# A modulated four-layer residual convolution: a block sum moved from GpSimd to VectorE, a scaled identity moved from VectorE to ScalarE

## The chip, the cores and the metric

The kernel runs on one core of one Trainium2 chip. The metric is device time in microseconds, the median of several executions. All work is in 32-bit floats.

## What is computed

The reference passes a batch of 128 samples (64 channels, 1024 columns) through four modulated convolutions and adds the input. Cut to what matters:

```
for i, typ in enumerate(('same', 'upsample', 'same', 'downsample')):
    s = style @ mw.T + mb
    weight = SCALE * w * s[:, None, :, None]
    demod = rsqrt(sum(weight * weight, axis=(2, 3)) + EPS)
    weight = weight * demod[:, :, None, None]      # one weight per sample
    out = conv(x, weight) + b                      # 3 taps; up and down with a blur
...
return x + out
```

## The kernel before

**One combined convolution per sample.** All four layers are linear, so the kernel multiplies the layers' weights of each sample into one chain on TensorE, and then applies one short convolution to the input; the ends of the rows are done apart. Samples go in quartets, 32 of them (q = 0 to 31). Four samples share a tile: two halves of the partitions times two positions in the free dimension. [...]

**The chain of a quartet.** `scale3` makes tile wd (third layer's weights, scaled). `stage1` multiplies it with the second-layer weights into PSUM tile psS, and ScalarE copies that, scaled by table tB, into tile S, which holds eight blocks (slots) of 64 columns. Quartets 0, 1, 2 and 6 use the plain `stage1`. The other 28 use `stage1_a` and `stage1_b`: five products by way of sums of neighbouring taps; ScalarE writes four slots, VectorE (L442) two more from PSUM, and GpSimd (L445) adds slot 0 to slot 2. `share_sums` (L462) adds slots pairwise. `stage2` multiplies S with the blurred first layer E into psR, in turns that share through `share`, `share_copy` and `stage2_rest`, with differences of E's taps in Ed; ScalarE copies the result as tile R (scaled by tC). `stage3` multiplies R with the zeroth layer into the tile W, called Wf in the profile, scaled by table t0. From quartet 6 it is split in `stage3_b` and `stage3_a`: after stage3_b ScalarE copies two blocks from psA to psW in four operations, then five blocks to Wf in two; stage3_a adds to psW, and ScalarE copies four blocks more.

**From the weights to the output.** `combine_a` and `combine_b` make on VectorE (all at L662, the helper `sum_of`) the three sums h1, h2, h3 of the weights, tile H in the profile. Between h1 and h3 `residual` (L659) adds to one tap, for each half r, the identity matrix divided by three, idn3, times the sample's entry of table t3: this is the `x +` of the reference. `combine_a` makes h1, the residual, and h3; `combine_b` h2, h1, and h2 again. `product` (L753) does the convolutions: conv3 needs only h3, conv1 and conv2 need h1 and h2, conv4 and conv0 need W itself. Input sums T and G come from VectorE and GpSimd. ScalarE copies conv3's result (m3), VectorE makes y1 (`sum1`) and the third outputs Y (`sum2`: first Y = 3 m3 + psA, in one operation for each of two PSUM banks, then y1 less psA). conv4 then adds to Y. `output` scales on ScalarE, SyncE's queue stores.

**The order of the work** is written out by hand and kept: each engine executes its instructions in the order of the program. `early_turn` serves q = 0 to 3, `turn_of` q = 4 to 28, and the last three quartets stand at the end. Turn q finishes quartet q, makes the combined weights of n = q + 1 and the chain of c = q + 2. In `turn_of` the order is stage2(c), conv2(q), sum2(q), stage3_b(c), combine_a(n), conv4(q), stage3_a(c), combine_b(n), conv3(n), outputs, copies, conv0(q), conv1(n). In the first of these turns (q = 4, entry) sum2, conv4 and combine_a(n) stand ahead of stage3_b, and r_sums(c) (L588) on VectorE behind combine_a. In the turn at q = 29 it is stage2, conv2, stage3 part 0, sum2's first step, combine_a(n), conv4, conv3. In an early turn it is stage2(c), sum2(q), combine_a(n), conv4(q), stage3(c, 0), conv3(n).

Of the kernel before, what the change touches and what calls it, by code (L numbers as in the profile page):

```python
# [63 lines left out]
def kernel(  # L64
# [199 lines left out]
    def var_newton(bs, ls=slice(0, NL)):  # L264
# [4 lines left out]
    ALT, ODD, DOWN = slice(0, 4, 2), slice(1, 4, 2), (slice(3, 4), slice(1, 2))  # L269
    tA, tB, tBn, tC, t0, t3, td, tb = (  # L270
        const.tile([P, NQ, 2], F32, name=n) for n in ("tA", "tB", "tBn", "tC", "t0", "t3", "td", "tb")
    )
# [20 lines left out]
    def table_B(bs):  # L293
        table(nc_g, tB, bs, ALT, DOWN, sc[:, 2, bs], sc[:, 1, bs])

    def table_Bn(bs):
        qs = slice(bs.start // 4, bs.stop // 4)
        nc_g.tensor_scalar_mul(tBn[:, qs], tB[:, qs], -1.0)

# [65 lines left out]
    w3x = const.tile([P, 5, C], F32, name="w3x")  # L365
    w2n = const.tile([P, 5, C], F32, name="w2n")

    def split_weights():
        nc_g.tensor_copy(w3x[:, :K], w3)
        nc_g.tensor_scalar_mul(w2n[:, :K], woi[2], -1.0)  # L370
        for t, src in ((w3x, w3), (w2n, woi[2])):
            nc_g.tensor_add(t[:, K:], src[:, : K - 1], src[:, 1:])

# [30 lines left out]

    EVEN = slice(0, K, 2)

    def stage1(q, pool=None, engs=(nc_a, nc_a), between=None):

        wd = chain[q]
        ps = unit(pool or ps_w, f"psS{q}")  # L410
        for k, (at, at1) in enumerate(((0, 3), (3, 1), (1, 4))):
            tap_matmul(ps, wd, at, 2, woi[2][:, k, :], EVEN, first=k == 0)
            tap_matmul(ps, wd, at1, 1, woi[2][:, k, :], slice(1, 2), last=k == K - 1)
        if between:
            between()
        st, _ = s_tiles(q)
        for r in range(2):
            scaled_copy(engs[r], flat(st[r][:, 1:6]), ps[r][:, : 5 * C], tB[:, q, r : r + 1])
        chain[q] = st
        return ps  # L420

    def stage1_a(q, ps=None):

        ps = ps or unit(ps_w, f"psS{q}")
        wd = chain[q]
        tap_matmul(ps, wd, 2, 2, w2n[:, 0, :], EVEN, first=True)
        tap_matmul(ps, wd, 3, 2, w2n[:, 2, :], EVEN)
        tap_matmul(ps, wd, 1, 1, w2n[:, 1, :], slice(1, 2))
        st, t = s_tiles(q)
        for r in range(2):  # L430
            scaled_copy(nc_a, flat(st[r][:, :4]), ps[r][:, C : 5 * C], tBn[:, q, r : r + 1])
        chain[q] = wd, ps, st, t

    def stage1_b(q):

        wd, ps, st, t = chain[q]
        tap_matmul(ps, wd, 2, 1, w2n[:, 3, :], slice(3, 4))
        tap_matmul(ps, wd, 4, 1, w2n[:, 4, :], slice(4, 5), last=True)
        for r in range(2):
            p1 = st[r][:, 0:1, :].to_broadcast([P, 2, C])  # L440
            sums = ps[r][:, 2 * C : 6 * C].rearrange("c (a b o) -> c a b o", a=2, b=2)[:, :, 0]
            nc_v.scalar_tensor_tensor(  # L442
                st[r][:, 4:6, :], sums, tB[:, q, r : r + 1], p1, op0=ALU.mult, op1=ALU.subtract
            )
        nc_g.tensor_add(t[:, :, 2], t[:, :, 2], t[:, :, 0])  # L445
        chain[q] = st
        whole[q] = t
# [5 lines left out]
    def tap_differences():  # L453

        d = Ed[:, :4].rearrange("c (a b) o -> c a b o", a=2)
        for b in range(2):
            nc_g.tensor_sub(d[:, :, b], E[:, 4 * b : 4 * b + 5 : 4], E[:, 2:7:4])
        nc_g.tensor_sub(Ed[:, 4:], E[:, 3:8:4], E[:, 5:6].to_broadcast([P, 2, C]))

    def share_sums(q):  # L460
        t = whole[q]
        nc_v.tensor_add(t[:, :, 6:8], t[:, :, 1:5:3], t[:, :, 2:6:3])  # L462

# [12 lines left out]
    def share(q, ps):  # L476

        at = [NB + 4 + i * C for i in range(3)]
        p12, p34 = ([b[:, i:j] for b in ps] for i, j in zip(at, at[1:]))
        chain_matmul(p12, E[:, 2], chain[q], slice(6, 7))  # L480
        chain_matmul(p34, E[:, 6], chain[q], slice(6, 7))
        chain_matmul(p34, E[:, 5], chain[q], slice(7, 8), True)
        shared_ps[q] = [b[:, at[0] : at[2]] for b in ps]
# [12 lines left out]
    def stage2_rest(q):  # L496
# [4 lines left out]
        plan = (  # L501
            (apart, E[:, 0], slice(1, 4, 2)),
            (block(1), Ed[:, 0], slice(2, 3)),
            (block(2), Ed[:, 1], slice(1, 2)),
            (block(3), E[:, 2], slice(3, 4)),
            (block(3), Ed[:, 2], slice(2, 3)),
            (block(4), Ed[:, 3], slice(1, 2)),
            (block(4), E[:, 4], slice(3, 4)),
            (block(5, 2), E[:, 8], slice(2, 4)),
            (block(5), E[:, 6], slice(3, 4)),  # L510
            (block(1, 2), E[:, 1], slice(4, 6)),
            (block(2), E[:, 3], slice(4, 5)),
            (block(3), Ed[:, 4], slice(5, 6)),
            (block(4), Ed[:, 5], slice(4, 5)),
            (block(5), E[:, 7], slice(5, 6)),
        )
# [4 lines left out]
    def stage2(q, pool=None, engs=(nc_a, nc_a), between=None):  # L521
# [3 lines left out]
        for n, e in enumerate(() if shared else (-2, -1, 0, 1, 2, 3, 4, 5, 6)):  # L525
            if e % 2 == 0:
                a, lo, m = slice(1, 4), e // 2 + 1, 3
            else:
                a, lo, m = slice(4, 6), (e + 3) // 2, 2
            for r, rows in enumerate(HALF):  # L530
                for c, cols in enumerate(HALF):
                    src = st[c if r == 0 else 1 - c]
                    nc.tensor.matmul(  # L533
                        ps[r][cols, lo * C : (lo + m) * C],
                        E[rows, e + 2, :],
                        src[rows, a, :],
# [90 lines left out]
    def stage3(q, part, pool=None, engs=(nc_a, nc_a)):  # L627
# [24 lines left out]
        return ps  # L652

    def residual(q):

        W = Wq[q][0]
        for r in range(2):
            v = W[:, tap(1, 1), r, :]
            nc_v.scalar_tensor_tensor(v, idn3, t3[:, q, r : r + 1], v, op0=ALU.mult, op1=ALU.add)  # L659

# [207 lines left out]
    w0s = [woi[0]] + [const.tile([P, K, C], F32, name=f"w0s{i}") for i in range(2)]  # L868
    idn3 = const.tile([P, C], F32, name="idn3")

    def scaled_weights():
# [308 lines left out]
    stage3(0, 1, ps_conv, BOTH)  # L1180
    const_first(0, first)
    stage1(2)
    combine_a(0)
# [21 lines left out]
    for of in (table_B, vector_a1, table_0, vector_b1, vector_c2):  # L1205
        of(PART[1])
    table_Bn(slice(0, PART[1].stop))
    stage3(1, 1)
# [38 lines left out]
    def layers(i, j):  # L1247
# [5 lines left out]
        (2, 1): lambda: (small_rest(2), var_root(REST, Y[:, 0])),  # L1253
        (2, 2): lambda: (table_B(REST), table_Bn(REST), vector_a1(REST)),
        (3, 0): lambda: (var_newton(*layers(2, 3)), var_newton(*layers(0, 2))),
# [381 lines left out]
```

## Time and profile before

| what | value |
|---|---|
| median of 3 runs | 479.15 us (478.75 to 479.64) |
| profiled execution, its own time from first to last instruction | span 478.0 us |
| the median less that span | 1.15 us |
| share of the span: TensorE, VectorE, ScalarE, GpSimd | 98%, 87%, 65%, 34% |
| TensorE, convolutions psA from T and H (L753) | 2304 passes, 187.3 us |
| VectorE, residual (L659) | 64 operations, 16.9 us, 304 ns each |
| GpSimd, sum in S (L445) | 28 operations, 22.1 us, 790 ns each |
| VectorE, sums from PSUM into S (L442) | 56 operations, 16.8 us, 341 ns each |

PE in the profile is TensorE's matrix work, PEld its loading of weights, DVE VectorE, ACT ScalarE and POOL GpSimd. A row of the timeline has the start, the length, the engine, the line, the operation with what it writes and reads, and the count of merged rows; in brackets stands how long the engine had been idle and who released it. A row of the groups has the total busy time, the mean of one in ns, and then the idle time before. Neighbouring operations of one engine overlap a little, so two of 0.31 us can start 0.21 apart.

### The profile page before, as it was taken

How to read it: one execution, taken by the hardware profiler on the slowest of the kernel's cores; microseconds unless marked ns; L12 is line 12 of the kernel's file. 1: busy time of each engine (PE TensorE's matmuls, PEld its weight loads, DVE VectorE, ACT ScalarE, POOL GpSimd, SP SyncE). 2: the span in 40 equal slices, each digit the busy share in tenths (PEclk: the TensorE clock that was granted, in tenths of full speed). 3: DMA queues.
4: the chain of work that ended last, by engine and by line, in shares of the span. 5: the costliest groups of instructions: out<-in, count | busy, mean ns of one | idle time of the engine just before them, and what ended most of it. 6: DMA issues, size and time to landing. Idle time of an engine off the chain costs nothing.

```text
span 478.0 us, 26721 instructions
## 1 busy us (share of the span) xinstructions
PE 469.6 (98%) x11928; PEld 346.4 (72%) x11928; DVE 417.5 (87%) x690; ACT 310.1 (65%) x708; POOL 163.5 (34%) x197
## 2 busy tenths in 40 slices
PE   8999999999999999999999999999999999999995
PEld 7877788777878876677776677766887777766652
DVE  5889998879889998899979899979989999999895
ACT  5565666667666676666667666667666768766352
POOL 3434032663335342243432233422434432333200
PEclk9999999999999999999999999999999999999998
DMA  5406365544445554345543455533455554445125
GB/s 175 158 28 200 114 195 192 150 139 144 139 150 157 173 173 127 122 151 160 171 149 120 131 170 152 173 127 126 145 169 162 162 154 146 152 146 170 61 91 191
DMA packets 50514, 70.70 MB, mean 148 GB/s; under 512 B 5664, under 2 KB 47328, under 8 KB 50400
## 3 DMA queue, kind: packets, MB, share of 16 engines
q1 hardware_dynamic: 49808, 68.32, 45.8%
q8 instruction: 93, 1.52, 1.5%
q10 hardware_dynamic: 592, 0.69, 0.5%
q14 instruction: 21, 0.17, 0.1%
HBM read 35.36 MB, written 33.62 MB: 144 GB/s over the span
## 4 chain that ended last, share of the span: by engine, by line
PE 95%; DVE 4%; issue 0%; ACT 0%; ACTq 0%; DVEq 0%
PE psA L753 45%; PE Y L753 11%; PE psR L467 9%; PE psA L571 7%; PE psW L571 7%; PE psS L389 6%; PE psR L533 4%; PE psA L467 2%; PE Y L994 2%; DVE H L662 1%; PE Y L180 1%; PE Y L336 1%; DVE G L662 0%; PE psM L204 0%; DVE o L832 0%
## 5 line engine op out<-in xcount | busy, mean ns | idle before, releaser
L753 PE MATMUL psA<-T,H 64*64 64x340 f32 x2304 | 187.3, 447 | 0.8 <-DVE y L662 0.7
L753 PEld LDWEIGHTS psA<-T,H 64*64 64x64 f32 x2304 | 89.9, 133 | 50.0 <-issue 3.1
L662 DVE SCALAR_TENSOR_TENSOR G<-X 128x1376 f32<-128x1376 f32 (+2 forms) x65 | 78.1, 1207 | 1.1 <-DMA X<-in_x 0.9
L726 POOL TENSOR_TENSOR T<-G 128x684 f32<-128x684 f32 x28 | 46.5, 1659 | 73.1 <-DVE G L662 73.1
L445 POOL TENSOR_TENSOR S<-S 128x128 f32<-128x128 f32 x28 | 22.1, 790 | 144.1 <-ACT S L360 136.8
L360 ACT ACTIVATE R<-psR,tC 128x448 f32<-128x448 f32 x63 | 36.5, 630 | 46.3 <-PE psR L467 26.7
L753 PE MATMUL psA<-T,Wf 64*64 64x340 f32 x768 | 63.9, 446 | 0.0
L753 PE MATMUL Y<-T,Wf 64*64 64x340 f32 x768 | 62.8, 451 | 0.1
L662 DVE SCALAR_TENSOR_TENSOR Y<-m,psA 128x340 f32<-128x340 f32 x64 | 33.1, 517 | 28.0 <-PE psA L753 26.6
L360 ACT ACTIVATE psW<-psA 128x128 f32<-128x128 f32 x100 | 19.3, 269 | 50.3 <-PE psA L571 46.2
L740 DVE TENSOR_TENSOR T<-G 128x1368 f32<-128x1368 f32 (+1 forms) x33 | 50.7, 1540 | 0.0
L360 ACT ACTIVATE Wf<-psW,t 128x256 f32<-128x256 f32 (+2 forms) x76 | 32.7, 479 | 26.5 <-PE psW L571 26.2
L711 DVE TENSOR_TENSOR T<-X 128x684 f32<-128x684 f32 x32 | 47.9, 1496 | 0.0
L467 PE MATMUL psR<-S,E 64*64 64x64 f32 (+1 forms) x1472 | 46.5, 238 | 0.0
L731 POOL TENSOR_TENSOR T<-G 128x684 f32<-128x684 f32 x28 | 46.5, 1660 | 0.0
L389 PEld LDWEIGHTS psS<-wd,w2n 64*64 64x64 f32 x1120 | 35.0, 133 | 13.3 <-ACT S L360 0.8
L467 PEld LDWEIGHTS psR<-S,E 64*64 64x64 f32 x1472 | 39.6, 134 | 5.2 <-ACT psR L490 0.2
L753 PEld LDWEIGHTS Y<-T,Wf 64*64 64x64 f32 x768 | 29.6, 132 | 18.0 <-DVE Y L662 0.7
L830 ACT ACTIVATE o<-psA,tb,td 128x340 f32<-128x340 f32 x63 | 37.0, 647 | 6.3 <-PE psA L753 6.3
L753 PEld LDWEIGHTS psA<-T,Wf 64*64 64x64 f32 x768 | 29.1, 133 | 15.1
L830 ACT ACTIVATE o<-Y,tb,td 128x340 f32<-128x340 f32 x63 | 36.6, 637 | 4.5 <-PE Y L753 2.7
L830 ACT ACTIVATE o<-y,tb,td 128x340 f32<-128x340 f32 x62 | 38.5, 679 | 0.6 <-DVE y L812 0.6
(165 smaller groups left out, 832.4 us busy)
## 6 DMA issues: line engine op xcount, KB each, us to landing
out<-o SPq DMA_DIRECT2D x167, 170.0 KB, 2.6
X<-in_x SPq DMA_DIRECT2D x150, 172.0 KB, 3.6
X<-in_x SPq DMA_DIRECT2D x14, 516.0 KB, 5.3
out<-o SPq DMA_DIRECT2D x6, 510.0 KB, 5.4
out<-o SPq DMA_DIRECT2D x2, 340.0 KB, 3.0
Xe<-in_x_ends SPq DMA_DIRECT2D x1, 512.0 KB, 6.7
out<-o ACTq DMA_DIRECT2D x3, 170.0 KB, 2.3
par<-in_params SPq DMA_DIRECT2D x2, 192.0 KB, 3.4
```

Source lines behind the costliest of these rows:

```text
L360: nc_a.activation(dst, src, AF.Copy, scale=f)
L389: nc.tensor.matmul(ps[r][cols, at * C : (at + n) * C], weight[rows], wd[c if r == 0 else 1 - c][rows, taps], start=first, stop=last, skip_ ...
L445: nc_g.tensor_add(t[:, :, 2], t[:, :, 2], t[:, :, 0])
L467: nc.tensor.matmul(dst[r][cols], weight[rows], st[c if r == 0 else 1 - c][rows, slots, :], start=False, stop=last, skip_group_check=True,)
L571: nc.tensor.matmul(dst[r][cols], weight[rows], t[rows, c, slots, :], start=first, stop=last, skip_group_check=True,)
L662: nc_v.scalar_tensor_tensor(out, x, f, y, op0=ALU.mult, op1=op)
L711: nc_v.tensor_sub(t[:, pairs, 0, :NJ], plane(X, 3, pairs), plane(X, 1, pairs))
L726: eng.tensor_add(t[:, :, 0, :NJ], plane(g, 2), plane(g, 1))
L731: eng.tensor_sub(t[:, :, 1, :NJ], plane(g, 2), plane(g, 1))
L740: nc_v.tensor_sub(t[:, pairs, :, :NJ], both(a, PL), both(b, 1))
L753: nc.tensor.matmul(ps[s][cols, :NB], w, Ts[q, tag][rows, c, i, g : g + NB], start=(g == 0 and m == 3), stop=(g == K - 1), skip_group_check ...
L830: nc_a.activation(dst, src, AF.Identity, bias=add, scale=d3)
```

## The change

Four things are edited.

1. **S's middle block.** `stage1_a` no longer uses negated weights and the negated table tBn; it writes the slots 0, 2, 4, 6 with tB. `stage1_b` uses negated sums w2n (now two blocks), and its VectorE operation makes three slots, 3 to 5, of 192 columns, in place of two. GpSimd's addition is gone. The odd slots stay negated, and the products of stage2 that read them use negated odd taps En; all slot numbers change, the number and sizes of the products do not.
2. **The plain stage1** multiplies all three taps of wd in one go (192 columns) instead of two and one. Its odd slots are not negated, so stage2 uses E for those quartets.
3. **The residual.** A new function `identity` makes x3, 128 columns, on ScalarE in two operations of 64, from idn3 and t3. It is called at the head of `combine_a` (for q = 0 a little earlier). `residual` is one addition of 128 columns on VectorE. x3 is one tile for all quartets.
4. **sum2's first step** is one operation over both banks where the two lie in one tile.

```
+    w2n = const.tile([P, 2, C], F32, name="w2n")
+    En = const.tile([P, 4, C], F32, name="En")
...
+        nc_g.tensor_add(w2n, woi[2][:, : K - 1], woi[2][:, 1:])
+        nc_g.tensor_scalar_mul(w2n, w2n, -1.0)
+
+    def negated_taps():
+        nc_g.tensor_scalar_mul(En, E[:, 1:8:2], -1.0)
...
-        for k, (at, at1) in enumerate(((0, 3), (3, 1), (1, 4))):
-            tap_matmul(ps, wd, at, 2, woi[2][:, k, :], EVEN, first=k == 0)
-            tap_matmul(ps, wd, at1, 1, woi[2][:, k, :], slice(1, 2), last=k == K - 1)
+        plain.add(q)
+        for k in range(K):
+            tap_matmul(ps, wd, k, K, woi[2][:, k, :], slice(0, K), first=k == 0, last=k == K - 1)
...
-            p1 = st[r][:, 0:1, :].to_broadcast([P, 2, C])
-            sums = ps[r][:, 2 * C : 6 * C].rearrange("c (a b o) -> c a b o", a=2, b=2)[:, :, 0]
+            p1 = st[r][:, 0:1, :].to_broadcast([P, K, C])
+            sums = ps[r][:, 2 * C : 5 * C].rearrange("c (a o) -> c a o", o=C)
             nc_v.scalar_tensor_tensor(
-                st[r][:, 4:6, :], sums, tB[:, q, r : r + 1], p1, op0=ALU.mult, op1=ALU.subtract
+                st[r][:, 3:6, :], sums, tB[:, q, r : r + 1], p1, op0=ALU.mult, op1=ALU.add
             )
-        nc_g.tensor_add(t[:, :, 2], t[:, :, 2], t[:, :, 0])
...
-        nc_v.tensor_add(t[:, :, 6:8], t[:, :, 1:5:3], t[:, :, 2:6:3])
+        nc_v.tensor_add(t[:, :, 1:8:6], t[:, :, 2:4], t[:, :, 4:6])
...
-            (block(1, 2), E[:, 1], slice(4, 6)),
-            (block(2), E[:, 3], slice(4, 5)),
+            (block(1, 2), En[:, 0], slice(3, 6, 2)),
+            (block(2), En[:, 1], slice(3, 4)),
...
+    def identity(q):
+        for r in range(2):
+            nc_a.activation(x3[:, r], idn3, AF.Copy, scale=t3[:, q, r : r + 1])
+
     def residual(q):
-        W = Wq[q][0]
-        for r in range(2):
-            v = W[:, tap(1, 1), r, :]
-            nc_v.scalar_tensor_tensor(v, idn3, t3[:, q, r : r + 1], v, op0=ALU.mult, op1=ALU.add)
+        v = Wq[q][0][:, tap(1, 1)]
+        nc_v.tensor_add(v, v, x3)
...
     def combine_a(q):
         chain.pop(q)
+        if q:
+            identity(q)
         a, b, c, h1, h2, h3 = taps(q)
         sum_of(h1, c, -2.0, a)
         residual(q)
...
-            for s, a in enumerate(banks(q)):
-                sum_of(Y[:, s, :NB], m3[:, s], 3.0, a[:, :NB])
+            for s, a in parts(q):
+                sum_of(Y[:, s, :NB], m3[:, s], 3.0, a)
```

More of the change, by code (lines that the diff above doesn't have):

```diff
@@ L405 @@
     EVEN = slice(0, K, 2)
+    plain = set()
     def stage1(q, pool=None, engs=(nc_a, nc_a), between=None):
@@ L501, in stage2_rest @@
         plan = (
[L502 to L510, printed above, removed]
-            (block(1, 2), E[:, 1], slice(4, 6)),
-            (block(2), E[:, 3], slice(4, 5)),
+            (apart, E[:, 0], slice(2, 7, 4)),
+            (block(1), Ed[:, 0], slice(4, 5)),
+            (block(2), Ed[:, 1], slice(2, 3)),
+            (block(3), E[:, 2], slice(6, 7)),
+            (block(3), Ed[:, 2], slice(4, 5)),
+            (block(4), Ed[:, 3], slice(2, 3)),
+            (block(4), E[:, 4], slice(6, 7)),
+            (block(5, 2), E[:, 8], slice(4, 7, 2)),
+            (block(5), E[:, 6], slice(6, 7)),
+            (block(1, 2), En[:, 0], slice(3, 6, 2)),
+            (block(2), En[:, 1], slice(3, 4)),
             (block(3), Ed[:, 4], slice(5, 6)),
-            (block(4), Ed[:, 5], slice(4, 5)),
-            (block(5), E[:, 7], slice(5, 6)),
+            (block(4), Ed[:, 5], slice(3, 4)),
+            (block(5), En[:, 3], slice(5, 6)),
         )
@@ L526, in stage2 @@
             if e % 2 == 0:
-                a, lo, m = slice(1, 4), e // 2 + 1, 3
+                a, lo, m, w = slice(2, 7, 2), e // 2 + 1, 3, E[:, e + 2]
             else:
-                a, lo, m = slice(4, 6), (e + 3) // 2, 2
+                a, lo, m = slice(3, 6, 2), (e + 3) // 2, 2
+                w = E[:, e + 2] if q in plain else En[:, (e + 1) // 2]
             for r, rows in enumerate(HALF):
@@ L1181 @@
     const_first(0, first)
+    identity(0)
     stage1(2)
@@ L1206 @@
         of(PART[1])
-    table_Bn(slice(0, PART[1].stop))
+    negated_taps()
     stage3(1, 1)
```

40 lines of the change are left out of this document (18 added, 22 removed).

## The prediction

> **What bounds the kernel now.** I read the page first, its shares, its clock row and its chain of waits:
>
> ```profile
> PE 469.6 (98%) x11928; PEld 346.4 (72%) x11928; DVE 417.5 (87%) x690; ACT 310.1 (65%) x708; POOL 163.5 (34%) x197
> PEclk9999999999999999999999999999999999999998
> PE 95%; DVE 4%; issue 0%; ACT 0%; ACTq 0%; DVEq 0%
> ```
>
> TensorE is busy for 98% of the span, at a clock that is full in all but the last slice, and 95% of the chain lies on it. So an edit pays only where it takes work from TensorE or a wait in front of it, and it costs wherever it puts a wait in front of it. Time won on VectorE, ScalarE or GpSimd is worth nothing by itself. Next I looked, in the timeline, at the part of one ordinary turn in which the changed operations stand (columns: start, length, engine, line, operation, count, and the idle time before it):
>
> ```profile
> 279.34 1.07 DVE L662 SCALAR_TENSOR_TENSOR Y<-m,psA 128x340 f32<-128x340 f32 x2 [0.76 <-PE psA L753]
> ...
> 280.15 0.21 PEld L571 LDWEIGHTS psA<-R,par 64*64 64x64 f32 x8
> ...
> 280.46 1.35 PEld L753 LDWEIGHTS Y<-T,Wf 64*64 64x64 f32 x24
> ...
> 280.73 0.77 ACT L360 ACTIVATE psW<-psA 128x128 f32<-128x128 f32 x4 [1.90 <-PE psA L571]
> 281.09 0.57 DVE L662 SCALAR_TENSOR_TENSOR H<-Wf 128x384 f32<-128x384 f32 x1
> 281.37 0.97 ACT L360 ACTIVATE Wf<-psA,t 128x320 f32<-128x320 f32 x2
> 281.59 0.47 DVE L659 SCALAR_TENSOR_TENSOR Wf<-idn,t,Wf 128x64 f32<-128x64 f32 x2
> ...
> 282.09 0.56 DVE L662 SCALAR_TENSOR_TENSOR H<-H,Wf 128x384 f32<-128x384 f32 x1
> ...
> 282.77 0.26 PEld L571 LDWEIGHTS psW<-R,w0s 64*64 64x64 f32 x8
> ...
> 282.94 1.36 PEld L753 LDWEIGHTS psA<-T,H 64*64 64x64 f32 x24
> ...
> 283.27 0.84 ACT L360 ACTIVATE Wf<-psW,t 128x256 f32<-128x256 f32 x2 [0.93 <-PE psW L571]
> ```
>
> In this stretch TensorE runs stage3_b of quartet c (until about 280.4), conv4 (weights from 280.46), stage3_a (its last weights at 282.77) and conv3 of quartet n (weights from 282.94), one straight after the other. Beside it VectorE makes the weights of conv3 in three operations: h1 at 281.09, the residual pair at 281.59 (L659), h3 at 282.09, which ends at 282.65. conv3 starts 0.29 us later, so its weights are in time, but only just. ScalarE, at the same moment, is at work for the *other* quartet c: four copies at 280.73, then two scaled ones that end at 281.37 + 0.97 = 282.34. It cannot start them earlier, since it waited 1.90 us for stage3_b of TensorE.
>
> **The change, part by part.** *The residual.* Before, L659 reads a table and needs nothing fresh from ScalarE. Now it adds x3, and ScalarE writes x3 in the same turn. The kernel's order decides how late. On ScalarE, in an ordinary turn, stood (psA, psW and Wf of quartet c):
>
> ```order
> L360 ACTIVATE psW_0_4723<-psA_4692 128x2x64
> L360 ACTIVATE psW_1_4724<-psA_4692 128x2x64
> L360 ACTIVATE Wf_4693<-psA_4692,t_137 128x5x64 x2
> L360 ACTIVATE Wf_4693<-psW_0_4723,t_137 128x4x64
> L360 ACTIVATE Wf_4693<-psW_1_4724,t_137 128x4x64
> ```
>
> and now (x_156 is x3, idn_155 the scaled identity):
>
> ```order
> L356 ACTIVATE psW_0_4660<-psA_4629 128x2x64
> L356 ACTIVATE psW_1_4661<-psA_4629 128x2x64
> L356 ACTIVATE Wf_4630<-psA_4629,t_136 128x5x64 x2
> L658 ACTIVATE x_156<-idn_155,t_137 128x64 x2
> L356 ACTIVATE Wf_4630<-psW_0_4660,t_136 128x4x64
> L356 ACTIVATE Wf_4630<-psW_1_4661,t_136 128x4x64
> ```
>
> The two identities of quartet n stand behind all copies of stage3_b of quartet c. On VectorE the residual keeps its place between h1 and h3; before:
>
> ```order
> L662 SCALAR_TENSOR_TENSOR Y<-m_16_4802,psA_4692 128x340 x2
> L812 TENSOR_TENSOR y_16_4887<-y_16_4887,psA_4692 128x680
> L662 SCALAR_TENSOR_TENSOR H_4694<-Wf_4693 128x384
> L659 SCALAR_TENSOR_TENSOR Wf_4693<-idn_155,t_138,Wf_4693 128x64 x2
> L662 SCALAR_TENSOR_TENSOR H_4694<-H_4694,Wf_4693 128x384
> ```
>
> and now:
>
> ```order
> L666 SCALAR_TENSOR_TENSOR Y<-m_16_4740,psA_4629 128x2x340
> L818 TENSOR_TENSOR y_16_4824<-y_16_4824,psA_4629 128x680
> L666 SCALAR_TENSOR_TENSOR H_4631<-Wf_4630 128x384
> L663 TENSOR_TENSOR Wf_4630<-Wf_4630,x_156 128x128
> L666 SCALAR_TENSOR_TENSOR H_4631<-H_4631,Wf_4630 128x384
> ```
>
> So a new chain leads to conv3: stage3_b on TensorE, six copies on ScalarE, two identities, the addition, h3, conv3. Queued behind the waiting addition are h3, the rest of combine_b and the turn's input sums; conv3 waits for h3, and everything that TensorE still has to do waits for conv3. The prices come from these rows:
>
> ```profile
> L462 DVE TENSOR_TENSOR S<-S 128x256 f32<-128x256 f32 x23 | 9.6, 418 | 0.0
> L255 DVE TENSOR_TENSOR nw<-dm,var 128x64 f32<-128x64 f32 x2 | 0.4, 222 | 0.0
> L442 DVE SCALAR_TENSOR_TENSOR S<-psS,tB,S 128x128 f32<-128x128 f32 x56 | 16.8, 341 | 5.4 <-ACT o L830 2.8 <-PE psS L389 2.3
> L360 ACT ACTIVATE psW<-psA 128x128 f32<-128x128 f32 x100 | 19.3, 269 | 50.3 <-PE psA L571 46.2 <-issue 4.1
> L662 DVE SCALAR_TENSOR_TENSOR Y<-m,psA 128x340 f32<-128x340 f32 x64 | 33.1, 517 | 28.0 <-PE psA L753 26.6
> L662 DVE SCALAR_TENSOR_TENSOR y<-psA,m 128x680 f32<-128x680 f32 x32 | 27.6, 862 | 7.4 <-PE psA L753 5.9 <-PE psW L571 1.3
> ```
>
> and from the timeline near the start of the kernel:
>
> ```profile
> 16.24 0.42 ACT L360 ACTIVATE Wf<-psW,t 128x192 f32<-128x192 f32 x1 [0.15 <-PE Y L914]
> 16.70 0.42 DVE L362 TENSOR_SCALAR Wf<-psW,t 128x192 f32<-128x192 f32 x1 [0.50 <-ACT Wf L360]
> ...
> 33.64 0.31 ACT L245 ACTIVATE dm<-Y,eps 128x64 f32<-128x64 f32 x1 [0.98 <-PE Y L232]
> 33.85 0.31 ACT L247 ACTIVATE var<-Y,eps 128x64 f32<-128x64 f32 x1
> ```
>
> Two 128x64 activations with a pointer operand start 0.21 us apart, so each identity moves the end on ScalarE by 0.21: the pair ends at 282.34 + 0.42 = 282.76. VectorE starts 0.04 after ScalarE's end (16.66 to 16.70). The addition of 128x128 lies between the 222 ns of 128x64 and the 418 ns of 128x256, on the line 0.29. h3 follows 0.03 later (282.06 to 282.09) and takes 0.56; weights are loaded 0.05 after VectorE's end (279.34 + 1.07 = 280.41 to 280.46). Sum: 282.34 + 0.42 + 0.04 + 0.29 + 0.03 + 0.56 + 0.05 = 283.73, against 282.94 now: **0.79 us of waiting in a turn**. Nothing hides it: all of TensorE's later work stands behind conv3, and the next turn's copies again start only when TensorE has done stage3_b, so no lead is carried over. The bounds: two identities at the 0.17 spacing of the four copies at 280.73 ((0.77 - 0.27) / 3), or a little under, 0.30, with an addition of 0.22, give 0.60; two without overlap, 0.62, and an addition of 0.34 (L442) give 1.04.
>
> The Trainium skill (ScalarE: Activation LUTs, section "What ACT_TABLE_LOAD costs") gives an ACTIVATE 186 ns + 0.833 ns an element, 93 ns more for a pointer operand, and 93 ns of overlap between neighbours. By that an identity is about 332 ns and a pair moves the end by 0.48 in place of 0.42, an estimate that would make the sum below 1.4 us larger; the rows have the nearest thing itself, so I keep 0.42.
>
> How many turns? There are 100 psW copies, four a turn, so 25 turns with stage3_b. In the first of them (entry) combine_a stands ahead of stage3_b, which leaves 24. The first and the last of these 24:
>
> ```profile
> 108.14 0.97 ACT L360 ACTIVATE Wf<-psA,t 128x320 f32<-128x320 f32 x2
> 109.72 0.21 PEld L753 LDWEIGHTS psA<-T,H 64*64 64x64 f32 x8
> ...
> 436.77 0.97 ACT L360 ACTIVATE Wf<-psA,t 128x320 f32<-128x320 f32 x2
> 438.34 0.79 PEld L753 LDWEIGHTS psA<-T,H 64*64 64x64 f32 x16
> ```
>
> From the copies' end to conv3 it is 0.61 and 0.60 us, as in the turn above. So 24 x 0.79 = **+19.0 us** (14.4 to 25.0).
>
> The entry turn and the last turn but two have other orders:
>
> ```profile
> 91.12 1.16 ACT L360 ACTIVATE R<-psR,tC 128x448 f32<-128x448 f32 x2 [2.31 <-PE psR L533]
> ...
> 92.31 0.46 DVE L588 TENSOR_TENSOR R<-R 128x256 f32<-128x256 f32 x1 [0.31 <-ACT R L360]
> ...
> 93.65 0.24 PEld L571 LDWEIGHTS psA<-R,par 64*64 64x64 f32 x8
> ...
> 450.90 1.05 ACT L360 ACTIVATE Wf<-psW,t 128x384 f32<-128x384 f32 x2 [2.02 <-PE psW L571]
> ...
> 452.12 1.01 PEld L753 LDWEIGHTS psA<-T,H 64*64 64x64 f32 x16
> ```
>
> At the entry, r_sums (L588) stands on VectorE behind combine_a. The identities end at 92.28 + 0.42 = 92.70, the addition and h3 at 93.62, r_sums about 0.46 later at 94.09, and the last weights of stage3_b that need it go at 94.14 instead of 93.65: **+0.5**. In the turn at 450 the copies end at 451.95; the same chain of 0.42 + 0.04 + 0.29 + 0.03 + 0.56 + 0.05 = 1.39 ends at 453.34 against 452.12: **+1.2**. In the early turns conv4 and a whole stage3 part stand between the copies of R and conv3, and hide it.
>
> *The third outputs' sum in one operation* (sum2): 0.86 in place of 1.07 us. conv4's weights now start 0.10 after the load before them ended (280.15 + 0.21 to 280.46), held by sum2, and this wait goes. What is late next is conv3's h3, whose chain hangs on stage3_b and not on conv4: nothing is gained, **0**, in these turns. If the residual did not wait, it would be worth 0.10 a turn.
>
> *S's middle block.* GpSimd's L445 goes; GpSimd is off the path. VectorE's L442 grows from 128 to 192 elements, 0.07 each by the slope from 517 to 862 ns over 340 elements, 0.13 a turn; with the residual's 0.47 to 0.29 and sum2's 0.21, VectorE's work falls by 0.26 a turn. It idles 26.6 us before sum2, some 1.0 in a turn; a turn longer by 0.79 and 0.26 less work make up for the 1.2 us that it waits in the residual. **0**, as long as that cover holds. TensorE's matrix products in stage1_a and stage1_b keep their number and size; En and the strided slots change what is read, not how much: 0.
>
> *The plain stage1* of four quartets goes from 48 passes to 24 of 192 columns:
>
> ```profile
> 12.65 1.23 PE L389 MATMUL psS<-wd,par 64*64 64x128 f32 x48
> 13.71 0.51 PE L571 MATMUL psW<-R,par 64*64 64x192 f32 x8
> ...
> 444.95 2.67 PE L533 MATMUL psR<-S,E 64*64 64x192 f32 x72
> 447.45 0.46 PE L753 MATMUL psA<-T,H 64*64 64x340 f32 x4
> ```
>
> Now 1.06 us each. The 72 passes of stage2 (40 of 192 columns, 32 of 128) take 2.50, 0.212 ns a column, so 24 x 192 columns take 0.98: 4 x 0.08 = **-0.3**. The negated taps on GpSimd are one small operation in place of another: 0.
>
> Sum: 19.0 + 0.5 + 1.2 - 0.3 = **+20.4 us**. The profiled span is 478.0, and the median of the runs 479.15 has 1.15 around it, which the change does not touch: 478.0 + 20.4 = 498.4 of span, **499.6 us**. With the bounds of the stall, 495.0 to 505.6.
>
> **The rivals.** *Faster (0.04):* ScalarE's identities are there before VectorE asks, so conv3 does not wait. Then conv4's wait goes as well: 25 x 0.10 + 0.3 = 2.8, 476.4 us. It decides where h3 ends before 282.89, that is with a chain of 0.55 behind the copies where h3 alone takes 0.56. For it speaks only that ScalarE has idle time; against it, the order, in which the identities stand behind copies that end at 282.34. That the order is not what runs is included here; no difference gets 0.01.
>
> *A smaller stall (0.06):* TensorE wins back in the same turn half of what it lost, from short waits for ScalarE or VectorE further on: 24 x 0.4 + 1.4 = 11.0, 490.2. Against it: 98% busy leaves little to win back.
>
> *VectorE becomes the bound (0.05):* its cover of about 0.85 a turn (1.0 + 0.79 + 0.26 - 1.2) is an average; if turns with extra work overrun it by 0.4, 24 x 0.4 = 9.6 more, 509.2.
>
> *The clock falls (0.02):* a TensorE that stops in every turn might be granted less. If it ran half of each turn (14.3 us, from 109.72 to 438.34 in 23 turns) at the lowest digit of the clock row, 8, that is 7.15 x 0.25 = 1.8 a turn, 43 us, 543. Against it, the clock row: waits such as the 0.10 us before conv4 stand in these turns now, and it stays at 9.
> By the Trainium skill (TensorE: Matmul & The Clock Gate, "A second HAM failure mode: psum-queue depth-cycling") frequent micro-idles between groups of matmuls can make the gate swing; its section on oscillation asks for idle gaps above about 3.4 us, which no wait here would reach.
>
> **The numbers.** The forecast has 0.82. A measurement of this kernel tells about 0.2% from no change. Range 490 to 507: the bounds of the stall, the smaller stall below, and part of an overrun of VectorE above. Faster 0.04, same 0.01, slower 0.95.
>
> **What would show it.** Right: in an ordinary turn conv3's weight load follows h3 by 0.05 and shows an idle time released by VectorE's H; the addition (L663) is released by ScalarE's x3; copies' end to conv3 is 1.39 instead of 0.60; TensorE's share falls from 98% to about 94%; conv4's weights no longer wait for sum2. Wrong in size: a pair of identities that moves the end by other than 0.42, or an addition other than 0.29. Wrong altogether: no wait in front of the addition, or the copies' end to conv3 unchanged.

## The result and the profile after

The changed kernel takes **507.31 us** (median; 506.52 to 510.67) against 479.25 us for the kernel before: a ratio of 1.0602 [1.0567, 1.0637]. It is slower, as forecast, and by more than forecast: 507.31 lies 0.3 us above the range. The profiled execution has a span of 504.8 us, 26.8 more than before.

The page of the changed kernel: busy shares, the clock row, the chain, and two groups of instructions (total busy, mean in ns, idle time before).

```profile
PE 474.6 (94%) x11832; PEld 363.9 (72%) x11832; DVE 411.4 (81%) x626; ACT 325.6 (65%) x772; POOL 138.0 (27%) x168
PEclk9999999999999999999999999999999999999999
PE 61%; ACT 10%; DVE 6%; issue 2%; DMA 0%; ACTq 0%; DVEq 0%
L759 PE MATMUL psA<-T,H 64*64 64x340 f32 x2304 | 188.4, 449 | 23.4 <-DVE H L666 19.0
L663 DVE TENSOR_TENSOR Wf<-Wf,x 128x128 f32<-128x128 f32 x32 | 9.4, 295 | 37.6 <-ACT x L658 37.6
```

TensorE is busy for 94% in place of 98%, and its clock row stays at 9. The chain that was TensorE's by 95% now runs over ScalarE (10%) and VectorE (6%) as well. The convolutions themselves kept their length (449 ns a pass; a pass is one matrix instruction of the profile), but 23.4 us of waiting stand in front of those that read H, 19.0 of it for H. The addition L663 waited 37.6 us for ScalarE's x3 over its 32 executions.

One ordinary turn of the changed kernel, from the timeline (start, length, engine, line, operation, count, and the idle time before it with its releaser):

```profile
294.95 0.24 PEld L573 LDWEIGHTS psA<-R,par 64*64 64x64 f32 x8
295.12 1.43 PEld L759 LDWEIGHTS Y<-T,Wf 64*64 64x64 f32 x24
...
296.20 0.97 ACT L356 ACTIVATE Wf<-psA,t 128x320 f32<-128x320 f32 x2
297.01 0.62 ACT L658 ACTIVATE x<-idn,t 128x64 f32<-128x64 f32 x2
...
297.67 0.29 DVE L663 TENSOR_TENSOR Wf<-Wf,x 128x128 f32<-128x128 f32 x1 [1.19 <-ACT x L658]
298.00 0.56 DVE L666 SCALAR_TENSOR_TENSOR H<-H,Wf 128x384 f32<-128x384 f32 x1
298.67 1.38 PEld L759 LDWEIGHTS psA<-T,H 64*64 64x64 f32 x24 [0.89 <-ACT Wf L356]
298.70 1.66 PE L759 MATMUL psA<-T,H 64*64 64x340 f32 x20 [0.78 <-DVE H L666]
```

The chain of the prediction can be read step by step. ScalarE copies stage3_b of quartet c until 297.17, then makes the pair of identities until 297.63. VectorE has waited 1.19 us and adds at 297.67. h3 runs from 298.00 to 298.56, and the weights of conv3 are loaded at 298.67. The idle time before that load is 0.89. Its releaser is given as ScalarE's Wf, which had long been there; the row of the matmuls below it names the right one, VectorE's H. From the copies' end to conv3 it is 1.50 us, where it was 0.60.

To see where the 26.8 us lie, I cut the span at the first weight load of conv3 of quartets 0, 4, 5, 6 and 29 (us; the starts of those loads in the timelines):

| stretch | before | after | difference |
|---|---|---|---|
| start to conv3 of quartet 0 | 19.53 | 20.87 | +1.34 |
| to quartet 4 | 59.07 | 58.54 | -0.53 |
| to quartet 5 | 17.30 | 20.36 | +3.06 |
| to quartet 6 | 13.82 | 15.12 | +1.30 |
| 23 turns to quartet 29 | 328.61 | 349.14 | +20.53 |
| to the end | 39.68 | 40.78 | +1.10 |

The middle turn of the 23 went from 13.84 to 14.76 us. These ordinary turns, with the one from 5 to 6, hold 21.83 us. The second place is the stretch from quartet 4 to 5: one turn, 3.06 us. The first row isn't taken as an effect of the change: in the profiled executions of all kernels below the start lies between 19.91 and 22.73, with no edit that it goes with. It goes with the speed of TensorE's first passes. A pass of 192 columns takes 0.52 us at first and 0.32 later, and the traces have the change at about 7.3 us in the kernel before (start 19.53), 10.1 in the changed one (20.87) and 14.1 in the slowest start (22.73).

The stretch from 4 to 5 begins in the turn of quartet 3. Before, the timeline has in that turn these rows:

```profile
85.26 0.23 DVE L927 TENSOR_SCALAR oc<-oc,par_s 128x16 f32<-128x16 f32 x1
85.41 0.86 DVE L662 SCALAR_TENSOR_TENSOR y<-psA,m 128x680 f32<-128x680 f32 x1
86.38 0.24 PEld L753 LDWEIGHTS psA<-T,H 64*64 64x64 f32 x8 [0.49 <-issue]
86.93 0.46 POOL L445 TENSOR_TENSOR S<-S 128x128 f32<-128x128 f32 x1 [11.73 <-ACT S L360]
87.35 1.65 POOL L726 TENSOR_TENSOR T<-G 128x684 f32<-128x684 f32 x1
```

and after the change:

```profile
77.57 0.58 ACT L658 ACTIVATE x<-idn,t 128x64 f32<-128x64 f32 x2
78.19 0.29 DVE L663 TENSOR_TENSOR Wf<-Wf,x 128x128 f32<-128x128 f32 x1 [1.95 <-ACT x L658]
...
87.29 1.67 POOL L732 TENSOR_TENSOR T<-G 128x684 f32<-128x684 f32 x1 [12.09 <-DVE G L666]
87.72 1.28 DVE L934 TENSOR_SCALAR oc<-oc,par_s 128x16 f32<-128x16 f32 x1
88.91 0.85 DVE L666 SCALAR_TENSOR_TENSOR y<-psA,m 128x680 f32<-128x680 f32 x1
89.88 0.24 PEld L759 LDWEIGHTS psA<-T,H 64*64 64x64 f32 x8 [3.08 <-POOL T L732]
```

VectorE waits 1.95 us in the residual of quartet 4. conv3 of that quartet doesn't notice, but all that VectorE does afterwards comes later, to the end of the turn: sum1 (the row y<-psA) starts at 88.91 in place of 85.41. sum1 reads the PSUM tile that conv2 of the same quartet overwrites at the end of this turn, and conv2's weights wait 3.08 us, where it was 0.49: they go 0.12 after sum1's end (88.91 + 0.85 = 89.76). The releaser in the row, GpSimd's T, ended only at 88.96, so both it and sum1 were late, and sum1 came last. Part of the delay, 1.05 us, has another origin: the small operation on oc (L927 before, L934 after) took 1.28 us in place of 0.23. Without the addition in S in front of it, GpSimd starts its T<-G before L934, where it came after it.

### The profile page after: what moved, and what is told of

It reads as the page before. It is cut to its first block, busy times and chain, and to the rows that moved or that the text cites. A ratio compares the mean times of both kernels' runs of the same rounds, so it can differ in the third digit from the quotient of the medians.

```text
span 504.8 us, 26498 instructions
## 1 busy us (share of the span) xinstructions
PE 474.6 (94%) x11832; PEld 363.9 (72%) x11832; DVE 411.4 (81%) x626; ACT 325.6 (65%) x772; POOL 138.0 (27%) x168
## 4 chain that ended last, share of the span: by engine, by line
PE 61%; ACT 10%; DVE 6%; issue 2%; DMA 0%; ACTq 0%; DVEq 0%
PE psA L759 36%; PE psR L468 9%; PE psA L573 6%; ACT Wf L356 4%; PE psS L389 4%; ACT psW L356 3%; DVE H L666 3%; ACT x L658 2%; PE psA L468 2%; PE Y L1001 2%; DVE Wf L663 1%; PE psR L535 1%; PE Y L759 1%; PE psW L573 1%; DMA out<-o 0%
## 5 line engine op out<-in xcount | busy, mean ns | idle before, releaser
L759 PE MATMUL psA<-T,H 64*64 64x340 f32 x2304 | 188.4, 449 | 23.4 <-DVE H L666 19.0
L759 PEld LDWEIGHTS psA<-T,H 64*64 64x64 f32 x2304 | 95.2, 133 | 70.4 <-ACT Wf L356 22.8
L356 ACT ACTIVATE S<-psS,tB 128x256 f32<-128x256 f32 (+1 forms) x63 | 26.8, 477 | 39.6 <-PE psS L389 39.6
L666 DVE SCALAR_TENSOR_TENSOR Y<-m,psA 128x680 f32<-128x680 f32 x32 | 27.9, 871 | 26.1 <-PE psA L759 26.0
L759 PEld LDWEIGHTS Y<-T,Wf 64*64 64x64 f32 x768 | 34.1, 133 | 13.0 <-DVE Y L666 0.5
L759 PEld LDWEIGHTS psA<-T,Wf 64*64 64x64 f32 x768 | 31.3, 133 | 13.3
L666 DVE SCALAR_TENSOR_TENSOR H<-Wf 128x384 f32<-128x384 f32 x64 | 40.5, 634 | 0.0
L663 DVE TENSOR_TENSOR Wf<-Wf,x 128x128 f32<-128x128 f32 x32 | 9.4, 295 | 37.6 <-ACT x L658 37.6
L666 DVE SCALAR_TENSOR_TENSOR H<-H,Wf 128x384 f32<-128x384 f32 x64 | 35.7, 558 | 2.2
```

What stands on the lines that cost most here:

```text
L356: nc_a.activation(dst, src, AF.Copy, scale=f)
L663: nc_v.tensor_add(v, v, x3)
L666: nc_v.scalar_tensor_tensor(out, x, f, y, op0=ALU.mult, op1=op)
L759: nc.tensor.matmul(ps[s][cols, :NB], w, Ts[q, tag][rows, c, i, g : g + NB], start=(g == 0 and m == 3), stop=(g == K - 1), skip_group_check ...
```

## The experiments

**Theories at the start.** Mine: the whole loss is the residual, and it is a loss of *place*, not of work: the identities stand on ScalarE behind copies that wait for TensorE. The rivals: part of the loss comes from S's block on VectorE; or the identities cost ScalarE's time wherever they stand; or VectorE as a whole has become the bound.

**1. The old residual, all else changed.**

```
 def residual(q):
-    v = Wq[q][0][:, tap(1, 1)]
-    nc_v.tensor_add(v, v, x3)
+    W = Wq[q][0]
+    for r in range(2):
+        v = W[:, tap(1, 1), r, :]
+        nc_v.scalar_tensor_tensor(v, idn3, t3[:, q, r : r + 1], v, op0=ALU.mult, op1=ALU.add)
 def combine_a(q):
-    if q:
-        identity(q)
```

> The residual is as it was before, on VectorE from the table; all else is as changed. Theory: the whole loss comes from the addition that waits for ScalarE's identity, so without it TensorE's waits before conv3 are gone, conv4's 0.10 us a turn goes too, and the time is 475.5 to 479.5 us. Rival (the new S block with its larger VectorE operation and strided slots has a price of its own): 483 to 490 us.

Measured: 477.89 us, ratio 0.9968 [0.9949, 0.9987]. The whole loss goes with the residual, and what is left of the change is a small gain. One place does not recover, though: the stretch from 4 to 5 is 19.70 here, against 17.30 before. Its timeline:

```profile
84.84 1.94 DVE L287 TENSOR_TENSOR tA<-sc,dm 64x48 f32<-64x48 f32 x2
85.07 1.65 POOL L732 TENSOR_TENSOR T<-G 128x684 f32<-128x684 f32 x1 [10.28 <-DVE G L668]
86.68 1.62 POOL L737 TENSOR_TENSOR T<-G 128x684 f32<-128x684 f32 x1
87.03 1.31 DVE L934 TENSOR_SCALAR oc<-oc,par_s 128x16 f32<-128x16 f32 x1
...
89.22 0.24 PEld L759 LDWEIGHTS psA<-T,H 64*64 64x64 f32 x8 [2.91 <-POOL tb L284]
```

Two steps of small VectorE operations ahead of sum1, the table tA (a row of two operations) and L934, take 1.94 and 1.31 us. Each ends with a GpSimd addition beside it: tA at 86.78 (GpSimd 86.72), L934 at 88.34 (GpSimd 88.30). conv2 waits 2.91 us behind sum1.

**2. The residual alone**, in the kernel before (`identity`, x3 and the new `residual`; S and sum2 as they were).

> The kernel before with the new residual alone (identity on ScalarE, one addition on VectorE), S, the plain stage1 and sum2 as before. Theory: the whole loss is here, and a little more than in the changed kernel, since the gains of the other parts (some 2 us) are missing: 507 to 510 us, with the same 0.9 us of waiting before conv3. Rival (the parts only cost together, the later VectorE operations of S and sum2 taking part in the wait): below 500 us.

Measured: 507.88 us, 1.0587 [1.0568, 1.0607]. The middle turn is 14.89 us long. With 1 this shows from both sides that the residual makes the loss. The stretch from 4 to 5 is 19.72, and here L934 has its old length:

```profile
87.63 0.23 DVE L932 TENSOR_SCALAR oc<-oc,par_s 128x16 f32<-128x16 f32 x1
...
88.75 0.24 PEld L757 LDWEIGHTS psA<-T,H 64*64 64x64 f32 x8 [2.00 <-POOL S L445]
```

So the wait before conv2 has two causes, and each is enough alone to lengthen it: the residual that VectorE waits for (2.00 us here), and the short operations beside GpSimd (2.91 in experiment 1).

**3. The other two parts alone**, each in the kernel before.

> The kernel before with only sum2's first step as one operation. Theory: the wait of 0.10 us before conv4 in each of 25 turns goes, and conv3's weights, ready 0.29 us ahead, do not take its place: 2.5 us less, 476.5 to 478 us. Rival (the wait lies under matrix products that still run, so nothing is won): no change, 479 to 480 us.

> The new S block and the new plain stage1 alone; residual and sum2 as before. Theory: GpSimd and VectorE are hidden and the plain stage1 saves 0.3 us at most: no change, 478.5 to 480 us. Rival (less work on GpSimd lets VectorE run freer and so shortens TensorE's waits): 2 us or more below the kernel before.

sum2 alone: 477.24 us, 0.9939 [0.9924, 0.9953]. The 23 turns take 325.79 us in place of 328.61, 0.12 a turn. In its timeline conv4's weights no longer wait, and all behind them moves up, in one ordinary turn:

```profile
279.11 0.23 PEld L571 LDWEIGHTS psA<-R,par 64*64 64x64 f32 x8
279.28 1.42 PEld L753 LDWEIGHTS Y<-T,Wf 64*64 64x64 f32 x24
...
280.36 0.97 ACT L360 ACTIVATE Wf<-psA,t 128x320 f32<-128x320 f32 x2
...
281.08 0.56 DVE L662 SCALAR_TENSOR_TENSOR H<-H,Wf 128x384 f32<-128x384 f32 x1
...
281.82 1.37 PEld L753 LDWEIGHTS psA<-T,H 64*64 64x64 f32 x24
```

conv4 at 279.28 follows directly on the load before it, and conv3 comes 0.49 after the copies' end (281.33) where it was 0.60. The chance that h3 would be late next isn't met either: h3 ends at 281.64, 0.18 before conv3.

S's block alone: 480.63 us, 1.0019 [0.9998, 1.0040], not to be told from no change, though 0.6 above the expected range. Two of its twelve executions, 483.39 and 485.51, had a mean granted clock of 0.993 and 0.994; the others had 0.996 to 0.999 and lie between 479.69 and 481.14. In the trace the 23 turns are 1.1 us shorter than before (327.50), and the stretch from 4 to 5 is longer, 18.37 in place of 17.30. There L934 is long again:

```profile
85.23 1.71 POOL L732 TENSOR_TENSOR T<-G 128x684 f32<-128x684 f32 x1 [10.49 <-PE psA L759]
85.67 1.30 DVE L934 TENSOR_SCALAR oc<-oc,par_s 128x16 f32<-128x16 f32 x1
86.88 0.85 DVE L668 SCALAR_TENSOR_TENSOR y<-psA,m 128x680 f32<-128x680 f32 x1
...
87.85 0.24 PEld L759 LDWEIGHTS psA<-T,H 64*64 64x64 f32 x8 [1.58 <-POOL T L732]
```

L934 ends at 86.97, 0.03 after GpSimd's addition, and conv2 waits 1.58 us for sum1 behind it. How much S's block costs in this turn hangs on which of VectorE's short operations fall beside GpSimd's additions: one here, two in experiment 1, one in the changed kernel. It and the residual don't add up either: +1.07 or +2.40 and +2.42 alone, +3.06 together.

sum2's gain does not show in the whole: the two other parts alone multiply to 1.0019 x 1.0587 = 1.0607, and the whole change measured 1.0602. The traces say the same. The 23 turns take 349.14 us in the changed kernel and 350.75 with the residual alone, 1.6 less, of which S's block alone gave 1.1; of the 2.8 us that sum2 alone gave there (328.61 to 325.79) hardly anything is left. It is lost in the wait, as the prediction's 0 for it had it.

**4. The same identities, earlier.** If place is the cause, the changed kernel with the identities of quartet n put at the head of each turn, before stage2(c), where ScalarE doesn't yet wait for stage3_b, must lose nothing:

```
 def combine_a(q):
-    if q:
-        identity(q)
...
+        identity(n)
         stage2(c)
```

The same line stands in early_turn and turn_of; for the last two quartets it goes before stage2 and behind conv3.

> The same two identities on ScalarE, but issued at the head of each turn, ahead of the copies of stage2, so that they stand before the copies of stage3_b in ScalarE's order. Theory: what costs is their place and not their work; the addition finds x3 ready, the distance from the copies' end to conv3 goes from 1.50 back to about 0.60, and the time is 475 to 479 us. Rival (two more activations a turn cost as such, wherever they stand): above 488 us.

Measured: 476.3 us, 0.9929 [0.9914, 0.9944]: no loss at all, and 0.7% below the kernel before. The number of operations on ScalarE is the same (772). One turn in the timeline:

```profile
259.05 0.58 ACT L658 ACTIVATE x<-idn,t 128x64 f32<-128x64 f32 x2
...
264.80 0.77 ACT L356 ACTIVATE psW<-psA 128x128 f32<-128x128 f32 x4 [1.95 <-PE psA L573]
...
265.60 0.28 DVE L663 TENSOR_TENSOR Wf<-Wf,x 128x128 f32<-128x128 f32 x1
```

The identities end at 259.63, 5.97 us before the addition, which has no wait in front of it any more. conv3's weights go 0.40 us after the copies' end (266.41 to 266.81). They lie in time that ScalarE idled away: it still waits 1.95 us for stage3_b.

**5. Which turns pay?** Two kernels with the identities early only from quartet 6 on (ahead_late), or only for quartets 1 to 5 (ahead_early).

In combine_a and in turn_of, for ahead_late:

```
-    if q:
+    if 0 < q <= 5:
         identity(q)
...
+        if not entry:
+            identity(n)
         stage2(c)
```

and for ahead_early, which has the call also before stage2(c) in early_turn:

```
-    if q:
+    if q > 5:
         identity(q)
...
+        if entry:
+            identity(n)
         stage2(c)
```

> The identities are issued ahead from quartet 6 on only; in the early turns and the entry turn they stay where the change put them. Theory: the 24 ordinary turns gain 0.92 each and the turn before the last two 1.3, in all 23, so 484 us; the wait of 3.1 us in the turn before the entry stays. Rival (that wait of 3.1 us was a consequence of something later or of chance): 480 us.

> The identities are issued ahead for quartets 1 to 5 only, the rest as changed. Theory: VectorE's wait of about 2 us in the turn before the entry goes, sum1 of quartet 4 is in time, the 3.1 us that TensorE waited there go back to about 0.5, and with the entry's 0.3 the time is 503.5 to 505 us. Rival (the 3.1 us come from GpSimd, as the profile names it, or from the other parts of the change): 506.5 to 508 us, with the wait still there.

ahead_late: 480.85 us, 1.0029 [1.0009, 1.0049]; the 23 turns take 325.36 us, all of their loss is gone (before the change it was 328.61), and the stretch from 4 to 5 is still long: 22.04, with the same 3.08 us before conv2. The expected 484 was too much.

Not all of these 22.04 us are the wait. The clock row of this run has a slice at 8, and conv2 stands in it:

```profile
PEclk9999999899999999999999999999999999999999
```

From 92.4 us on, 0.9 after conv2's weights at 91.52, the granted clock is 0.50 for 3.41 us. Half of that, 1.7 us, is my estimate of what it costs, and it is the difference to the changed kernel's 20.36, whose profiled execution has no such stretch. Seven of the ten executions of ahead_late, 480.39 to 483.49, had a mean granted clock of 0.993 to 0.996; the three others, 479.56 to 479.92, had 0.999 or 1.000. So of the 4.55 us between the medians of ahead_late and ahead_all, whose stretch from 4 to 5 takes 17.98, about 3.5 are the waits of the first quartets (479.81 against 476.30) and the rest goes with the clock.

ahead_early: 504.27 us, 1.0506 [1.0486, 1.0525]; the 23 turns take 348.83, as in the changed kernel (349.14), and the stretch from 4 to 5 falls from 20.36 to 18.00. It doesn't fall to 17.3, for the short operation beside GpSimd stays:

```profile
84.46 1.73 POOL L732 TENSOR_TENSOR T<-G 128x684 f32<-128x684 f32 x1 [10.22 <-DVE G L666]
84.91 1.31 DVE L934 TENSOR_SCALAR oc<-oc,par_s 128x16 f32<-128x16 f32 x1
...
87.11 0.24 PEld L759 LDWEIGHTS psA<-T,H 64*64 64x64 f32 x8 [1.22 <-POOL T L732]
```

L934 is still 1.31 us long (to 86.22, GpSimd to 86.19), and conv2 waits 1.22. I had expected 0.5 there.

**6. The pair of identities twice.** This measures the suspected chain by its price: a second pair, into a tile that nothing reads, ahead of the first.

```
-    for r in range(2):
-        nc_a.activation(x3[:, r], idn3, AF.Copy, scale=t3[:, q, r : r + 1])
+    for t in (x3b, x3):
+        for r in range(2):
+            nc_a.activation(t[:, r], idn3, AF.Copy, scale=t3[:, q, r : r + 1])
```

> The changed kernel with each identity issued twice, the first time into a tile that nobody reads: ScalarE has two more activations of 128x64 just ahead of those that count. Theory: they stand on the chain to conv3, so each pair adds the 0.42 to 0.50 us by which a pair moves ScalarE's end, 24 turns and the last one: 10 to 12.5 us more, 517 to 520 us. Rival (something else, such as the hand-over between engines, sets the wait): under 512 us.

```profile
305.29 0.62 ACT L659 ACTIVATE x3b<-idn,t 128x64 f32<-128x64 f32 x2
305.77 0.61 ACT L659 ACTIVATE x<-idn,t 128x64 f32<-128x64 f32 x2
...
306.41 0.29 DVE L664 TENSOR_TENSOR Wf<-Wf,x 128x128 f32<-128x128 f32 x1 [1.66 <-ACT x L659]
306.74 0.56 DVE L667 SCALAR_TENSOR_TENSOR H<-H,Wf 128x384 f32<-128x384 f32 x1
307.41 1.38 PEld L760 LDWEIGHTS psA<-T,H 64*64 64x64 f32 x24 [1.36 <-ACT Wf L356]
```

Measured: 521.27 us, 1.0858 [1.0835, 1.0881]. The second pair starts 0.48 after the first, VectorE's wait grows from 1.19 to 1.66 (+0.47), that of the weights from 0.89 to 1.36 (+0.47), and the middle turn from 14.76 to 15.23 (+0.47): what ScalarE takes there is paid by TensorE, 0.47 of 0.48. In the traces the 24 turns together grew by 10.5 us, of 14.0 between the two medians. In the stretch from 4 to 5 (22.81 in place of 20.36) the granted clock is 0.50 for 3.41 us from 91.6 on, again just behind a wait of 3.08 us before conv2; that is about 1.7 us, the same estimate as in 5. Both executions had a mean clock of 0.995 or 0.996, and without the 1.7 the time would lie in the expected 517 to 520.

**7. Can the turn of quartet 3 be mended?** In ahead_all conv2 still waits 1.19 us for sum1 behind a long L934 (1.31 us). With sum1 of quartet 4 put ahead of the tables and L934 on VectorE, that wait should go.

```
+        if twice:
+            sum1(n)
         extra(q, 1)
-        sum1(n)
+        if not twice:
+            sum1(n)
```

> The kernel with all identities ahead, and in the turn before the entry sum1 of quartet 4 issued on VectorE ahead of that turn's tables and of the 128x16 scalar operation on oc, which lasts 1.31 us there while GpSimd adds, against 0.23 in the kernel before. Theory: TensorE's wait of 1.19 us before conv2 of quartet 4 is sum1 standing behind that operation, so it falls to under 0.3 and the time is 0.7 to 1.2 us below the kernel with all identities ahead. Rival (TensorE waits for GpSimd's own addition, as the profile names it): the wait stays at about 1.2.

Measured: 476.57 us, 0.9941 [0.9921, 0.9961], not better than ahead_all. The stretch from 4 to 5 is 17.86 in place of 17.98. The wait before conv2 is gone, but the delay has moved to other operations on the same engine:

```profile
86.73 1.65 POOL L730 TENSOR_TENSOR T<-G 128x684 f32<-128x684 f32 x1 [10.24 <-DVE G L666]
87.98 2.08 DVE L287 TENSOR_TENSOR tA<-sc,dm 64x48 f32<-64x48 f32 x2
88.34 1.65 POOL L735 TENSOR_TENSOR T<-G 128x684 f32<-128x684 f32 x1
...
90.44 0.74 DVE L444 SCALAR_TENSOR_TENSOR S<-psS,tB,S 128x192 f32<-128x192 f32 x2
```

The two small table operations tA, 0.41 us in ahead_all, now lie beside GpSimd's two additions and take 2.08. They end at 90.06, after GpSimd's second one (89.99); the sums into S come later for it, and stage2's weights wait 0.80 us.

**8. The old S with the early identities.** The kernel before, with sum2's and the residual's change and the identities at the head of the turn.

> The kernel before with the new sum2 and the new residual with identities ahead; S's block with GpSimd's addition and the plain stage1 as before. Theory: the new S block gains nothing and only lets GpSimd start early enough to hold VectorE up in one turn; with the old one the operation on oc is back at 0.23 us, the wait before conv2 of quartet 4 at about 0.5, and the time is equal to the kernel with all identities ahead or up to 1 us below it. Rival (the new S block gains in the ordinary turns): 1 us or more above it.

```profile
84.51 0.23 DVE L930 TENSOR_SCALAR oc<-oc,par_s 128x16 f32<-128x16 f32 x1
...
85.63 0.30 PEld L755 LDWEIGHTS psA<-T,H 64*64 64x64 f32 x8 [0.27 <-issue]
86.39 0.46 POOL L445 TENSOR_TENSOR S<-S 128x128 f32<-128x128 f32 x1 [11.76 <-ACT S L360]
```

Measured: 475.6 us, 0.9925 [0.9901, 0.9949]. GpSimd is again busy with S only after L930, which is back at 0.23, and the stretch from 4 to 5 is 17.21. It has the lowest median of all, but ahead_all's interval covers it: what S's block is worth once the identities stand early is not settled by these runs.

## Why the prediction was right and where it was wrong

**What bounds the kernel, and the mechanism: right.** The loss is the new chain stage3_b, copies, identities, addition, h3, conv3, in 24 turns; experiments 1 and 2 place it in the residual, 4 in its position, and 6 shows that time added to this chain reaches the end. The predicted signs are all there: the wait of the addition for x3, that of conv3 for H, TensorE at 94%, conv4 no longer held by sum2.

**The ordinary turn: right in kind, too small.** Forecast 1.39 from the copies' end to conv3, measured 1.50: the pair of identities moved ScalarE's end by 0.46 where I had 0.42, h3 began 0.04 after the addition in place of 0.03, and conv3's weights followed h3 after 0.11 where I had 0.05; VectorE's start after ScalarE (0.04), the addition (0.29) and h3 (0.56) were as forecast. The 0.05 was read from conv4's load behind sum2; why h3 to conv3 takes 0.11, as in experiment 6 (307.30 to 307.41), no run tells. With 0.90 on the chain and 0.91 per turn measured (21.83 / 24), the term was 19.0 and should have been 21.8: 2.8 us of the miss. For the pair, two activations of 64 columns that read PSUM stood in for two that read a tile in SBUF. By the Trainium skill (ScalarE: Activation LUTs, section "What ACT_TABLE_LOAD costs") a pair would move the end by about 0.48, an estimate from its figures; the 0.46 here and the 0.48 between the pairs of experiment 6 agree with it, and the row that I had preferred was the worse guide: 24 x 0.04, 1.0 of the 2.8 us.

**"In the early turns conv4 and a whole stage3 part ... hide it": the step that failed.** For conv3 it held: conv3 of quartet 4 doesn't wait. But I followed the wait only to its first reader. VectorE executes in order, and behind its 1.95 us of waiting stood the input sums and sum1, for which conv2 at the end of the same turn waits, because it overwrites what sum1 reads. Experiment 2 shows this wait alone (2.00 us before conv2). The stretch from 4 to 5 grew by 3.06 where the entry had +0.5 in my sum; the wait that the 0.5 meant, that of stage3_b's last weights for r_sums, is there and is 0.28 us:

```profile
97.55 0.21 PEld L573 LDWEIGHTS psA<-R,par 64*64 64x64 f32 x8 [0.28 <-DVE R L590]
```

That is 2.6 us of the miss. The 0 for S's block, "as long as that cover holds", failed in the same turn: "GpSimd's L445 goes; GpSimd is off the path" counted what GpSimd no longer does, not what it now starts earlier. The rival "VectorE becomes the bound" had the right resource, but not the right place: no overrun is spread over the turns, as experiment 6 shows, where the middle turn grows by what the identities take and no more.

**The rest.** The turn near the end: +1.2 forecast, +1.10 measured. The plain stage1: -0.3 forecast, 0.08 a quartet. Its passes bear this out: from the first start to the last they take 0.88, 0.98 and 0.83 us in quartets 1, 2 and 6, where it was 1.02, 1.11 and 1.00. But the start and the stretch to quartet 4 together are 0.81 longer, 1.1 us of the miss. The forecast had no term for the slow first passes, which last 2.8 us longer in this execution; at 0.52 us for 0.32 that costs about 1.1, an estimate. The four parts, 2.8 + 2.6 + 1.1 - 0.1, make the 6.4 us between 20.4 and 26.8 of span. Another 1.3 or so lie outside it: the profiled execution had 1.8 us around its span (506.62 for 504.8) where I took 1.15, and the median of the runs is 0.7 above that execution. This last 0.7 goes with the clock: two of the four executions, 506.52 and 506.62, had a mean granted clock of 0.999 and 1.000 and lie inside the range, the two others, 508.00 and 510.67, had 0.996 and 0.993. So it hangs on the clock that the median lies 0.3 above the range; the 6.4 us of span are the error of the forecast. The range ended at 507 with "part of an overrun of VectorE"; a wait in one early turn was not in it.

**The other rivals.** The faster case (no wait, 476.4) is what ahead_all measured, 476.3, with the order that the prediction named as missing. The smaller stall didn't occur: nothing is won back later in a turn. The clock rival, 43 us lost in the ordinary turns, did not occur: in the profiled execution the clock row stays at 9 in all 40 slices, with a wait of 0.89 us in each turn. A small loss of that kind is real, as the clocks of the two longer executions show. ahead_late and identity_twice have a stretch at half clock just behind conv2's 3.08 us; the two longer executions left no trace, so where theirs lies, and whether the wait brings it about, is open.

## What to carry to other kernels

An operation that is moved to an engine with idle time takes its place in that engine's queue with it: ask what stands in front of it there and what that waits for, and put it where the engine is idle and nothing is awaited, since the same two operations cost 6% in one place and nothing 6 us earlier. Where an engine gets a new wait, follow all that is queued behind it to the end of the turn, not only the first reader. And when work is taken from an engine that is off the path, look at what it starts earlier, and beside whom.

## What the runs showed of the hardware

A short VectorE operation can take as long as a GpSimd addition beside it. L934 and its like (128x16) took 0.23 us where no GpSimd addition was running at their start (before, the residual alone, ahead_old_s) and 1.28 to 1.31 us beside the 1.62 to 1.73 us of GpSimd's T<-G (the changed kernel, the old residual, S's block alone, ahead_early), each time with its end 0.03 to 0.04 after GpSimd's; the two 64x48 table operations together took 1.94 and 2.08 beside such additions, and 0.41 where they had started first (ahead_all). sum1, which reads one operand from PSUM, kept its 0.85 to 0.87 beside them. The Trainium skill (SBUF — State Buffer, section "Who interferes with whom") says that VectorE and GpSimd share a pair of ports, and that a `tensor_scalar` of VectorE in a two-port mode can be blocked until the GpSimd operation is done, and that a VectorE instruction with two inputs in SBUF contends with a GpSimd operation that reads SBUF. These rows agree with it; that the ports are the cause was not tried apart, and in which mode L934 ran no view shows.

Small costs add up on a path of handovers: ScalarE to VectorE 0.04 us, VectorE to the weight load 0.11 (0.05 where conv4 followed sum2), and a pair of 64 columns on ScalarE 0.46 to 0.48.

The granted clock can halve for 3.41 us in the middle of a kernel: once in the traces of ahead_late (92.4 to 95.8 us) and identity_twice (91.6 to 95.0), 0.9 and 0.6 us after conv2's weights had ended a wait of 3.08 us. The changed kernel had the same wait and no such stretch in its profiled execution, and the old residual waited 2.91 there and had a mean clock of 0.997 or more in all twelve, so the wait alone does not decide it.
